# Fifth scan's decays in a tile outside layer 0's memory, second sequence's statistics ahead of the third scan, second gates in step 12, expert choice a scan later

## The chip, the core and the metric

The kernel runs on one core of a Trainium2 chip. A core has a matrix engine (TensorE, PE), a vector engine (VectorE, DVE), an engine for activation functions (ScalarE, ACT), a general engine (GpSimd, POOL) and one that mainly issues transfers (SyncE, SP). Each engine works through its own list of instructions in the order in which the program issues them; semaphores make an instruction of one engine wait for one of another. The metric is the time of one execution in device microseconds (us).

## The reference

The input x is four sequences of 256 tokens with 512 features, in float32. Two layers follow each other. Each adds to its input the sum of two branches, both fed with the layer norm of that input.

Layer 0: an attention with 32 heads over a latent of four numbers for each key, and a gated feed-forward with 1792 hidden features.

Layer 1: a selective state-space block and a mixture of experts.

```python
x, z = jnp.split(hidden_states @ in_proj_w, 2, axis=-1)
# causal convolution of four taps over time on x, then silu: xc
dt = softplus(dt_r @ dt_proj_w + dt_bias)          # dt_r, Bm, Cm: rms-normed projections of xc
h = exp(dt * A) * h + dt * Bm * xc                  # one step of time, 1024 channels x 16 states
y = sum over states of h * Cm
out = ((y + D * xc) * silu(z)) @ out_proj_w
```

The recurrence over h runs over 256 steps of time in each sequence. The expert part takes a softmax over eight experts for every token, keeps the two largest, and adds their low-rank products to a dense product.

## The kernel before

**Layer 0** is a list of TensorE work (attention and feed-forward) with the rest threaded between. Its last piece is the product of the hidden features with the down weights (`down`, L432). The generator `ff` holds this product for the last four blocks of 128 tokens; calls such as `go(ff, 9)` issue some of its matmuls at a time, so that the first steps of layer 1 run between them. The sums of the last three blocks stay in PSUM and are added to x by `add_last` (L452).

**Layer 1** works through the four sequences b = 0 to 3. Each sequence is cut into eight chunks of 128 channels (c), and each chunk into four groups of four states (g). So there are 32 steps for a sequence and 128 in all, counted by u. One step u handles 128 partitions x 4 x 256 elements:

- `decays(u)` (L877): four exponentials on ACT make the factors exp(dt * A) from the tile `dts` of the chunk.
- `scan_in(u)` (L891): DVE multiplies the spread rows of Bm with `dus` (dt times xc of the chunk) into `bx`, in PSUM, of which there is one buffer.
- `scan(u)` (L899): DVE runs the recurrence into `h`; GpSimd multiplies `h` with the rows of Cm into `hc`.
- `states_sum(u - 1)` (L919): TensorE sums `hc` over the states into `ysum`, one step later.
- `close_chunk` (L928), two steps after a chunk's last scan: DVE multiplies `ysum` with the gate `sz`.

The tiles `dts` and `dus` of a chunk come by way of a scratch tensor in HBM: `send` (L840) writes it, `spread` (L844) reads it back in the layout of the scan, both on SyncE's queue.

Around these steps stands everything that other sequences and chunks need, placed by hand. `put(b, s, f, ...)` (L1141) says that f is issued in step s of sequence b, ahead of that step's `scan_in`; `put_late` (L1144) places it after that step's `scan`. The loop at L1265 issues, for each u: the decays two steps ahead, what `put` placed, `scan_in`, `close_chunk`, `scan`, what `put_late` placed, and the sum of the step before. The order on each engine is the order of issue[...].

What the change touches:

- The decays' tiles. Steps 0 to 3 borrow memory: steps 0 and 2 use `decay[0]`, which lies in the pool `w1`, steps 1 and 3 use buffers of the weights (`lent`, L868). After the last matmul of `ff`, in step 2, `open_act` (L1123) closes layer 0's pools and opens the pool `act` in that memory, with two more decay tiles. From step 4 on `decay[u % len(decay)]` walks over the three. So step 4 takes `decay[1]` and step 5 `decay[2]`, both in the memory that layer 0 leaves. `decays(4)` is called at the end of step 2 (L1295), `decays(5)` at the start of step 3.
- The layer norm of the next sequence: `norm_stats` (L655: four instructions on DVE, then two small ones on ACT that make `rsn`), `norm_scale` (L665: `sh` on DVE, then two passes on ACT), `norm_turn`, `norm_copy`. For the second sequence the statistics stand late in step 3 and `norm_scale` in step 4 (L1209, L1210).
- The gates. `pz_mm(b, p, i)` (L852) multiplies with the z weights, `gate_silu` (L860) loads the table that has the silu, applies it to a pair of chunks and loads the table of exp and ln again. In the first sequence pair 1 has its matmuls in step 6 and its gate in step 8 (L1173, L1177).
- The step sizes dt: `step_in` (L772: `pdt` on TensorE, absolute value and relu on ACT) in steps 5 and 6 of the first sequence, `step_exp` (L787) in step 7.
- The next sequence's convolution: `px_mm` (L691), `conv_in` (L699: copy, first tap and three scaled copies on ACT), `conv_taps` (L716: three taps on DVE, three sums on GpSimd), pair after pair, two steps apart. In the first sequence the first pair's `conv_in` is in step 9, its taps in step 10.
- The weights' buffers: the tag `w_in` has three buffers that pairs of x and z weights use in turn; `load_x` and `load_z` (L1026, L1029) issue the transfers on SyncE's queue.
- The expert choice: `route_exp` (L962: maximum and difference on DVE, exp on ACT) in step 22 and `route` (L968: twenty small instructions on DVE) in step 23, of the first and third sequence, for two sequences at a time; `expert_turn` (L994: transposes on TensorE, a copy on ACT) in step 24, of the first three sequences.

Of the kernel before, what the change touches and what calls it, by code (L numbers as in the profile page):

```python
# [41 lines left out]
def block_kernel(  # L42
# [413 lines left out]
    def go(gen, n=1000):  # L456
        for _ in range(n):
            if next(gen, 1) == 1:
                break
# [169 lines left out]
    decay = []  # L629
# [210 lines left out]
    def send(n, b, p, t):  # L840
        live[n, b, p] = scr.tile([2, P, S], F32, tag=n, name=f"{n}d")
        nc.sync.dma_start(live[n, b, p].rearrange("c p t -> p c t"), t)
# [30 lines left out]
    def lend(n, u):  # L873
        tag = lent[n][u]
        return w1.tile([P, NG, S], F32, tag=tag, name=n, bufs=3 if tag == "w_in" else 1)

    def decays(u):  # L877
        b, c, g = u // PER, u % PER // NU, u % NU
        if u >= len(lent["d"]):
            da = decay[u % len(decay)]  # L880
        elif lent["d"][u] == "d":
            da = decay[0]
        else:
            da = lend("d", u)
            nc.gpsimd.memset(da[:, :, 0:1], 0.0)
        live["da", u] = da
        for k in range(NG):
            nc.scalar.activation(da[:, k, 1:], live["dts", b, c][:, k, 1:], AF.Exp,  # L888
                                 scale=aneg[:, c, k, g : g + 1])

    def scan_in(u):  # L891
        b, c, g = u // PER, u % PER // NU, u % NU
        bx = psx.tile([P, NG, S], F32, tag="bx", name="bx")
        nc.vector.tensor_tensor(  # L894
            bx, brow[g // 2][:, g % 2, :].unsqueeze(1).to_broadcast([P, NG, S]), live["dus", b, c], ALU.mult
        )
        live["bx"] = bx
# [191 lines left out]
    u, e, lw = live["u"], live["e"], live["lw"]  # L1089
# [51 lines left out]
    def put(b, s, f, *a):  # L1141
        at.setdefault(b * PER + s, []).append((f, a))

    def put_late(b, s, f, *a):  # L1144

        late_at.setdefault(b * PER + s, []).append((f, a))

    for b in range(B):
        nxt = b + 1
        if b:  # L1150
            put(b, 0, b_rows, b, 1)
            put(b, 0, spread, "du", b, 1)

            for c in range(DC):
                put(b, c // 2, out_mm, b - 1, 1, c)
            put(b, 3, out_x, b - 1, 1)
            put(b, 4, dense, b - 1, 0, 0)
            put(b, 5, dense, b - 1, 0, 1)
            put(b, 5, expert_out, b - 1, 0)
            for c in range(DC):  # L1160
                put(b, 6 + c, out_mm, b - 1, 0, c)
            put(b, 15, out_x, b - 1, 0)
        else:
            put(b, 1, one_out, 2)
            put(b, 1, one_step, 3)
            put(b, 2, one_out, 3)
            put_late(b, 2, load_z, b, 0)
            put_late(b, 2, lambda: send("dt", 0, 1, dts[0, 0][:, 2:4, :]))
            put_late(b, 2, step_x, b, 1)
            put(b, 4, load_z, b, 1)  # L1170
            for k, n in enumerate(("rl", "bw", "lb", "ow")):
                put(b, 9 + 2 * k, load_late, n)
            for p, u in ((0, 3), (1, 6)):  # L1173
                for i in range(2):
                    put(b, u, pz_mm, b, p, i)
            put(b, 4, gate_silu, b, 0)
            put(b, 8, gate_silu, b, 1)  # L1177
            put_late(b, 1, add_last, 5)
            put_late(b, 3, add_last, 6)
            put_late(b, 4, add_last, 7)  # L1180
        if b:
            put(b, 0, gate_silu, b, 0, 1)

        o = 0 if b else 3
        put(b, 1 if b else 5, step_in, b, 1, 0)
        put(b, 2 if b else 6, step_in, b, 1, 1)
        put(b, 3 if b else 7, step_exp, b, 1)
        for q in range(2):
            for k in range(3):
                put(b, 5 + o + 3 * q + k, step_out, b, 1, q, k)  # L1190
        for p in (2, 3):
            put(b, 3 * p + 2 + o, step_x, b, p)
        for c in range(2, DC):
            o = 0 if b or c < 4 else 1
            put(b, 3 if c == 2 and not b else 4 * c - 6 + o, spread, "dt", b, c)
            put(b, 4 * c - 4 + o, spread, "du", b, c)
        put(b, 10, load_z, b, 2)
        put(b, 12, load_z, b, 3)
        for p, at_i, at_g in ((2, (14, 15), 16), (3, (19, 21), 23)):
            for i in range(2):  # L1200
                put(b, at_i[i], pz_mm, b, p, i)
            if p == 3 or nxt == B:
                put(b, at_g, gate_silu, b, p)
        if nxt < B:
            o = 0 if b else 1
            if b:
                put(b, 0, norm_stats, nxt)
            else:
                put_late(b, 3, norm_stats, nxt)  # L1209
            put(b, 2 if b else 4, norm_scale, nxt)  # L1210
            put(b, 3 if b else 5, norm_turn, nxt, 0)
            (put if b else put_late)(b, 4 if b else 5, norm_copy, nxt, 0)
            put(b, 4 if b else 5, norm_turn, nxt, 1)
            (put if b else put_late)(b, 5, norm_copy, nxt, 1)
            for p in range(NP):
                put(b, 2 * p if b else (5, 6, 7, 8)[p], load_x, nxt, p)
                for i in range(2):
                    put(b, 6 + o + 2 * p + i, px_mm, nxt, p, i)
                put(b, 8 + o + 2 * p, conv_in, nxt, p)
                put(b, 9 + o + 2 * p, conv_taps, nxt, p)  # L1220
            put(b, 16 + o, conv_silu, nxt, (b, 2))
            put(b, 17 + o, pp_mm, nxt, 0)
            put(b, 18, pp_mm, nxt, 1)
            put(b, 19, pp_square, nxt)
            put_late(b, 20, pp_norm, nxt)
            put(b, 21, step_in, nxt, 0, 0)
            put(b, 22, step_in, nxt, 0, 1)
            put(b, 22, c_rows, nxt, 0)
            put(b, 23, step_exp, nxt, 0)
            put(b, 23, c_rows, nxt, 1)  # L1230
            for q in range(2):
                for k in range(3):
                    put(b, 24 + 3 * q + k, step_out, nxt, 0, q, k)
            put(b, 27, step_x, nxt, 0)
            put(b, 27, spread, "dt", nxt, 0)
            put(b, 29, spread, "du", nxt, 0)
            put(b, 30, step_x, nxt, 1)
            put(b, 30, b_rows, nxt, 0)
            put(b, 31, spread, "dt", nxt, 1)
            put(b, 23, load_z, nxt, 0)  # L1240
            put(b, 25, load_z, nxt, 1)
            for k, u in enumerate((27, 28, 29, 31)):
                put(b, u, pz_mm, nxt, k // 2, k % 2)
            if b % 2 == 0:
                for i, u in enumerate((16, 17, 18, 20)):
                    put(b, u, router, b, i)
                put(b, 22, route_exp, b)
                put(b, 23, route, b)
            put(b, 24, expert_turn, b)
            put(b, 25, dense, b, 1, 0)  # L1250
            put(b, 26, dense, b, 1, 1)
            put(b, 27, expert_out, b, 1)
        else:

            put(b, 12, expert_turn, b)
            put(b, 17, dense, b, 0, 0)
            put(b, 18, dense, b, 0, 1)
            put(b, 18, expert_out, b, 0)
            put(b, 20, dense, b, 1, 0)
            put(b, 21, dense, b, 1, 1)  # L1260
            put(b, 21, expert_out, b, 1)
# [3 lines left out]
    for u in range(total + 2):  # L1265
        if 3 <= u < total - 2:
            decays(u + 2)
        for f, a in at.get(u, ()):
            f(*a)
        if u < total:  # L1270
            if u:
                scan_in(u)
        last = u - 2
        if last >= 0 and last % NU == NU - 1:
            c = last % PER // NU
            close_chunk(last // PER, c)
            if last // PER == B - 1:
                late.append(c)
        if u < total:
            scan(u, 1 if u < total - 1 else 4)  # L1280
            if u < 2:
                decays(u + 2)
        for f, a in late_at.get(u, ()):
            f(*a)
        if late and u >= total - PER + 22:
            c = late.pop(0)
            for i in range(2):
                out_mm(B - 1, i, c)
        if 1 <= u <= total:
            states_sum(u - 1)  # L1290
        if u < 3:
            go(ff, (9, 12, 100)[u])
        if u == 2:
            open_act()
            decays(4)  # L1295
    for i in range(2):
        for c in late:
            out_mm(B - 1, i, c)
# [102 lines left out]
```

## Time and profile before

| what | value |
|---|---|
| time, median of three runs | 897.78 us (896.25 to 897.81) |
| time of the profiled execution | 898.7 us |
| its span, first to last instruction | 896.9 us |
| PE, DVE busy | 752.1 us (84%), 685.5 us (76%) |
| ACT, POOL busy | 526.3 us (59%), 490.3 us (55%) |
| scans on DVE (L909) | 129 instructions, 288.0 us |
| products bx on DVE (L894) | 128 instructions, 157.6 us |
| first scan starts at | 361.6 us |

The profile is of one execution, taken on the chip. Times in it are counted from the first instruction. In a row of a timeline stand the start, the length, the engine, the line of the program, the operation, the tile that it writes and those that it reads, the shapes, how many equal instructions are merged in the row, and in brackets how long the engine had been idle before it and what ended that. A matmul of float32 shows as two passes. The share of busy time is an average: TensorE leads it through layer 0, VectorE through most of layer 1.

### The profile page before, as it was taken

How to read it: one execution, taken by the hardware profiler on the slowest of the kernel's cores; microseconds unless marked ns; L12 is line 12 of the kernel's file. 1: busy time of each engine (PE TensorE's matmuls, PEld its weight loads, DVE VectorE, ACT ScalarE, POOL GpSimd, SP SyncE). 2: the span in 40 equal slices, each digit the busy share in tenths (PEclk: the TensorE clock that was granted, in tenths of full speed). 3: DMA queues.
4: the chain of work that ended last, by engine and by line, in shares of the span. 5: the costliest groups of instructions: out<-in, count | busy, mean ns of one | idle time of the engine just before them, and what ended most of it. 6: DMA issues, size and time to landing. Idle time of an engine off the chain costs nothing.

```text
span 896.9 us, 10459 instructions
## 1 busy us (share of the span) xinstructions
PE 752.1 (84%) x3554; PEld 433.4 (48%) x3554; DVE 685.5 (76%) x675; ACT 526.3 (59%) x1009; POOL 490.3 (55%) x377
## 2 busy tenths in 40 slices
PE   5999979999989999986885898687898768975875
PEld 3675545667556576653552444343444434422421
DVE  4595554376664423876998999999999989999996
ACT  4225445312437447588677596777686795764661
POOL 4222222001223242547966879868789749797664
PEclk9899999999999999998896999988999888899997
DMA  6232242001123141454752544432636332436200
GB/s 211 60 94 72 71 118 71 12 1 36 48 53 88 48 118 22 131 149 132 229 115 64 156 131 112 135 100 86 166 118 161 86 84 70 118 100 169 85 25 23
DMA packets 67343, 86.67 MB, mean 97 GB/s; under 512 B 12077, under 2 KB 52025, under 8 KB 66906
## 3 DMA queue, kind: packets, MB, share of 16 engines
q1 hardware_dynamic: 57930, 67.12, 26.8%
q0 software_dynamic: 9072, 18.35, 7.4%
q8 instruction: 28, 0.46, 0.2%
q10 hardware_dynamic: 288, 0.52, 0.2%
q14 instruction: 25, 0.20, 0.1%
HBM read 66.58 MB, written 10.22 MB: 86 GB/s over the span
## 4 chain that ended last, share of the span: by engine, by line
PE 39%; DVE 36%; ACT 14%; issue 5%; POOL 4%; DMA 1%; DVEq 0%; ACTq 0%; POOLq 0%
DVE h L909 21%; DVE bx L894 7%; ACT decay L888 6%; PE po L442 5%; PE pu L417 5%; PE pg L417 4%; PE sc L329 4%; PE av L371 3%; PE scT L361 3%; POOL hc L913 2%; PE pz L857 2%; PE pp L740 2%; PE px L696 2%; PE ysum L925 1%; ACT pe L363 1%
## 5 line engine op out<-in xcount | busy, mean ns | idle before, releaser
L913 POOL TENSOR_TENSOR hc<-h,cr 128x1024 f32<-128x1024 f32 (+1 forms) x131 | 302.3, 2310 | 115.1 <-DVE h L909 102.2
L909 DVE TENSOR_TENSOR_SCAN h<-decay,bx 128x1024 f32<-128x1024 f32 (+1 forms) x129 | 288.0, 2234 | 11.7
L888 ACT ACTIVATE decay<-dts,aneg 128x255 f32<-128x255 f32 x504 | 213.8, 498 | 126.4 <-DVE h L909 114.0
L925 PE MATMUL ysum<-hc,stack 128*32 128x256 f32 x1024 | 89.5, 420 | 91.5 <-POOL hc L913 91.2
L894 DVE TENSOR_TENSOR bx<-brow,dus 128x1024 f32<-128x1024 f32 x128 | 157.6, 1231 | 3.7
L429 POOL TENSOR_TENSOR hlo<-g,hhi 128x512 fp32r<-128x512 f32 x28 | 36.2, 1294 | 149.1 <-ACT hhi L428 149.1
L331 DVE TENSOR_REDUCE mpl<-sc 128x4 f32<-128x1024 f32 x64 | 77.2, 1222 | 24.1 <-PE sc L329 24.0
L925 PEld LDWEIGHTS ysum<-hc,stack 128*32 128x32 f32 x1024 | 21.7, 112 | 151.8 <-POOL hc L913 131.2
L400 POOL DMA_DIRECT2D wgu<-in_wgu x56 | 31.2, 558 | 92.5 <-PE pg L417 82.3
L363 ACT ACTIVATE pe<-scT 128x1024 f32<-128x1024 f32 x64 | 62.8, 1023 | 29.9 <-PE scT L361 29.6
L1017 PE MATMUL po<-ow,xc 128*128 128x512 f32 x128 | 71.2, 666 | 2.7 <-DVE xc L929 2.7
L857 PE MATMUL pz<-xn1T,w_in 128*128 128x256 f32 x256 | 68.5, 415 | 0.3 <-ACT dt L785 0.3
L696 PE MATMUL px<-xn1T,w_in 128*128 128x256 f32 x256 | 65.8, 406 | 0.8 <-DMA w_in<-in_inx 0.7
L696 PEld LDWEIGHTS px<-xn1T,w_in 128*128 128x128 f32 x256 | 51.4, 204 | 21.1 <-issue 11.0
L425 DVE SCALAR_TENSOR_TENSOR g<-g,pg 128x512 f32<-128x512 f32 x28 | 19.2, 685 | 52.0 <-ACT g L424 52.0
L857 PEld LDWEIGHTS pz<-xn1T,w_in 128*128 128x128 f32 x256 | 49.3, 202 | 19.0 <-issue 11.1
L428 ACT CAST hhi<-g 128x512 fp32r<-128x512 f32 x28 | 17.3, 620 | 61.9 <-DVE g L427 61.6
L417 PE MATMUL pg<-xhi,wgu 128*128 128x512 f32 x112 | 46.7, 417 | 5.4 <-issue 2.9
L417 PE MATMUL pu<-xhi,wgu 128*128 128x512 f32 x112 | 47.7, 426 | 3.1 <-issue 1.5
L442 PE MATMUL po<-wd,hhi 128*128 128x512 f32 x112 | 48.5, 433 | 0.0
L329 PE MATMUL sc<-km,qg 128*128 128x512 f32 x128 | 43.9, 424 | 3.3 <-ACT pe L363 2.8
L417 PE MATMUL pg<-xlo,wgu 128*128 128x512 f32 x112 | 44.9, 401 | 0.0
(225 smaller groups left out, 1255.2 us busy)
## 6 DMA issues: line engine op xcount, KB each, us to landing
dts<-dtd SPq DMA_DIRECT2D x124, 128.0 KB, 2.9
dus<-dud SPq DMA_DIRECT2D x124, 128.0 KB, 2.9
wgu<-in_wgu POOLq DMA_DIRECT2D x56, 256.0 KB, 2.7
w_in<-in_inz SPq DMA_DIRECT2D x16, 512.0 KB, 4.8
w_in<-in_inx SPq DMA_DIRECT2D x15, 512.0 KB, 4.3
dtd<-dt SPq DMA_DIRECT2D x15, 256.0 KB, 2.2
dud<-du SPq DMA_DIRECT2D x15, 256.0 KB, 2.3
wd<-in_wd POOLq DMA_DIRECT2D x7, 512.0 KB, 3.6
```

The costliest lines, as they stand in the source:

```text
L329: mm(sc[:, hp, :], lhsT=qs[b][:, gq, hf, qb * P : (qb + 1) * P], rhs=kms[b][:, 2 * hp : 2 * hp + 2, :], start=True, stop=True)
L331: nc.vector.tensor_reduce(mpl2[b % 2][:, qb, :, 16 + 2 * gq + hf].rearrange("p (a i) -> p a i", a=2), sc.rearrange("p a (i k) -> p a i k", ...
L363: nc.scalar.activation(pes[b, k][:, 2 * t : 2 * t + 2, :], sc, AF.Exp)
L417: mm(ps, lhsT=wgus[i][:, hc, :], rhs=xs[j][:, hc, :], start=(hc == 0 and j == 0), stop=(hc == HC - 1 and j == 1))
L442: mm(po, lhsT=hids[th][j][:, m, i * P : (i + 1) * P], rhs=wd[:, m, :], start=False, stop=(m == MC - 1 and j == 1))
L696: mm(px[:, i, :], lhsT=w[:, i, hc, :], rhs=xns[b][:, hc, :], start=(hc == 0), stop=(hc == HC - 1))
L857: mm(pz[:, i, :], lhsT=w[:, i, hc, :], rhs=xns[b][:, hc, :], start=(hc == 0), stop=(hc == HC - 1))
L888: nc.scalar.activation(da[:, k, 1:], live["dts", b, c][:, k, 1:], AF.Exp, scale=aneg[:, c, k, g : g + 1])
L894: nc.vector.tensor_tensor(bx, brow[g // 2][:, g % 2, :].unsqueeze(1).to_broadcast([P, NG, S]), live["dus", b, c], ALU.mult)
L909: nc.vector.tensor_tensor_scan(h[:, n].rearrange("p n t -> p (n t)"), da[:, n].rearrange("p n t -> p (n t)"), bx[:, n].rearrange("p n t -> ...
L913: nc.gpsimd.tensor_tensor(hc[:, n], h[:, n], crows[b][:, g, :].unsqueeze(1).to_broadcast([P, NG // parts, S]), ALU.mult,)
L925: mm(ysum[k * NB : (k + 1) * NB, :], lhsT=stack, rhs=hc[:, k, :], start=False, stop=(g == NU - 1))
```

## The change

The program computes the same with the same instructions; their places differ.

- From step 4 on the decay tiles are walked so that step 4 takes `decay[0]`, step 5 `decay[1]`, step 6 `decay[2]`. `decays(4)` is called a little earlier in step 2, after its scan, by the condition `u < 3`, and the call after `open_act` goes.
- The second sequence's statistics move from late in step 3 to the head of step 2.
- In the first sequence the matmuls of the second pair's gates move from step 6 to step 8, and their silu from step 8 to step 12.
- The loads of the next sequence's x weights, pairs 2 and 3, move from steps 7 and 8 to step 9, in the first sequence.
- The expert choice moves from step 23 to 24, the transposes behind it from 24 to 25.

```diff
     def decays(u):
         b, c, g = u // PER, u % PER // NU, u % NU
         if u >= len(lent["d"]):
-            da = decay[u % len(decay)]
+            da = decay[(u - 4) % 3]
...
-            for p, u in ((0, 3), (1, 6)):
+            for p, u in ((0, 3), (1, 8)):
                 for i in range(2):
                     put(b, u, pz_mm, b, p, i)
             put(b, 4, gate_silu, b, 0)
-            put(b, 8, gate_silu, b, 1)
+            put(b, 12, gate_silu, b, 1)
...
-            if b:
-                put(b, 0, norm_stats, nxt)
-            else:
-                put_late(b, 3, norm_stats, nxt)
+            put(b, 0 if b else 2, norm_stats, nxt)
...
-                put(b, 2 * p if b else (5, 6, 7, 8)[p], load_x, nxt, p)
+                put(b, 2 * p if b else (5, 6, 9, 9)[p], load_x, nxt, p)
...
-                put(b, 23, route, b)
-            put(b, 24, expert_turn, b)
+                put(b, 24, route, b)
+            put(b, 25, expert_turn, b)
...
             scan(u, 1 if u < total - 1 else 4)
-            if u < 2:
+            if u < 3:
                 decays(u + 2)
...
             open_act()
-            decays(4)
```

## The prediction

> **What bounds the kernel now.** I read the page's slices first: TensorE is full up to about 40% of the span (layer 0), VectorE from about 45% to the end. Then the waits of VectorE (DVE) from 355 us on, then the timelines of DVE and ScalarE (ACT) around them. I call the scans 0 to 127 by their step; "decays n" are the four exponentials that scan n reads. From step 4 on a step is one product bx (1.23 us) and one scan (2.29 us), and they follow each other every 3.65 us; so an idle microsecond of DVE there is a microsecond of the end, unless another wait takes its place.
>
> The waits of DVE from 355 us: who waits for whom, sum, times, longest.
>
> ```profile
> DVE sh L668 <- ACT rsn L652: 8.8, 1, 8.8
> DVE px L720 <- ACT xc L707: 7.0, 1, 7.0
> DVE xc L929 <- PE ysum L925: 3.8, 3, 2.3
> DVE w L956 <- ACT ex L966: 3.0, 2, 1.6
> ```
>
> Three of these four concern lines that the change moves. The timelines (start, length, instruction, idle time before it and its releaser) show what each stands on. ACT at the seam of the layers:
>
> ```profile
> 382.75 3.30 ACT L888 ACTIVATE decay<-dts,aneg 128x255 f32<-128x255 f32 x8 [9.81 <-PE po L442]
> 385.95 0.28 ACT L651 ACTIVATE rsn<-mv,eps 128x2 f32<-128x2 f32 x1
> 386.26 0.20 ACT L652 ACTIVATE rsn<-rsn 128x2 f32<-128x2 f32 x1
> 386.37 1.69 ACT L888 ACTIVATE decay<-dts,aneg 128x255 f32<-128x255 f32 x4
> 388.08 1.28 ACT L863 ACT_TABLE_LOAD   x1
> ...
> 400.70 0.47 ACT L784 ACTIVATE u<-pdt,vec 128x256 f32<-128x256 f32 x1 [2.31 <-PE pdt L779]
> ...
> 409.76 1.28 ACT L863 ACT_TABLE_LOAD   x1
> 411.06 0.60 ACT L863 ACTIVATE sz<-pz 128x512 f32<-128x512 f32 x1
> 411.67 1.28 ACT L647 ACT_TABLE_LOAD   x1
> 412.97 1.71 ACT L888 ACTIVATE decay<-dts,aneg 128x255 f32<-128x255 f32 x4
> ```
>
> DVE over the same stretch and at the expert choice:
>
> ```profile
> 386.50 0.16 DVE L668 SCALAR_TENSOR_TENSOR sh<-mv,rsn 128x2 f32<-128x2 f32 x1 [8.84 <-ACT rsn L652]
> 388.01 2.29 DVE L909 TENSOR_TENSOR_SCAN h<-decay,bx 128x1024 f32<-128x1024 f32 x1
> ...
> 416.34 1.01 DVE L720 SCALAR_TENSOR_TENSOR px<-pad,vec,px 128x256 f32<-128x256 f32 x2 [6.99 <-ACT xc L707]
> ...
> 472.50 0.20 DVE L956 TENSOR_REDUCE w<-ex 128x4 f32<-128x32 f32 x1 [1.57 <-ACT ex L966]
> ```
>
> ACT is idle 9.81 us because decays 4 go into a tile in layer 0's old memory, and layer 0's last product on TensorE (PE) ends just before 382.75. From there to the end of the first pair's convolution (xc, 416.30) ACT works almost without a pause while DVE waits 7 us for it: between 382.75 and 416.3 ACT is the bound, not DVE.
>
> [...] rsn's input was there at 377.66, and rsn ran at 385.95 behind decays 4 and 5. [...] Here the load is 1.28 us, but the next activation starts with it over (411.67+1.28 against 412.97)[...]; a gate costs 412.97 − 409.76 = 3.21 us, and I use that.
>
> **Part 1: decays 4 in the old tile, statistics ahead of scan 2.** The four statistics instructions (375.96 to 377.58, 1.62 us) now precede bx 2. Scan 2 goes from 369.49 to 371.1, scan 3 to 374.8 (ends 377.1), add, sh and bx 4 follow until 379.0. All this is inside DVE's idle stretch, so it costs nothing; without that cover it would cost 1.62. The rsn pair and decays 4 run on ACT from 372.94 (end of decays 3): rsn to 373.4, decays 4, free when scan 2 ends at 373.4, to 375.1. Thus 1.65 (half of 3.30) and 0.42 (385.95 to 386.37) leave the ACT chain that starts at 382.75. Decays 5 still wait there; from decays 7 on each waits, as before, for the scan three steps back.
>
> Scan 4 is not free at 379: its h is the first tile over layer 0's memory and in the built program waits for the same last product. It starts at 382.75 instead of 388.01. What is late next: chunk 0's product with its gate (L929). ACT does decays 5 and 6 (382.75 to 386.05), the table (1.28) and the silu (0.60): done at 387.94. So scan 5 starts at 388.3, against 392.26, and scans 6 to 8 follow at 3.65 each. This gain of 4 is no sum yet, as ACT decides again at the convolution.
>
> **Part 2: second gates in step 12, their matmuls in step 8.** From ACT's chain goes the gate, 3.21. Also its matmuls (16 passes, 395.89 to 399.61 on PE) no longer stand ahead of the second pdt, for which ACT waited 2.31. In the new order pdt follows the transposes (done by 392.1), one ysum and ACT's reading of the first pdt (393.8): done at 394.9, and ACT asks for it at 396.3. The wait goes whole.
>
> The matmuls now stand in step 8 ahead of the second half of px and ysum 7: ysum 5 to 395.5, px half to 397.5, ysum 6 to 398.1, gates 3.7 to 401.7, px half to 403.6, ysum 7 to 404.2. Chunk 1's product would have run at 402.8; it waits 1.4, and scan 9 ends at 406.8. ACT's chain is 1.65 + 0.42 + 3.21 + 2.31 = 7.59 shorter: xc ready at 416.30 − 7.59 = 408.7, still after DVE's 406.9. So the 1.4 is covered by 1.8, and the taps start 7.6 earlier.
>
> Loads: x pairs 2 and 3 take buffers that come free when those matmuls and the first px half end (401.7, and before 403.6). SyncE's queue now holds them behind the spread of dus for scans 12 to 15 (free to go when bx 7 ends, about 395.6) and rl; by the page's 4.3 us to landing they are there by 408. Pair 2 is used after the taps, past 410. Behind them stands dtd, whose data GpSimd finishes at about 411. Nothing is late.
>
> What step 12 pays: the gate stands between decays 14 and 15, where ACT idled 2.48 us for scan 12. 3.21 − 2.48 = 0.73 late; the third pair's xc was ready 0.33 before its taps (433.39 against 433.72): loss 0.4. The bounds are 0 (slack a little larger) and 3.2 (none). The silu itself is done some 1.8 us before chunk 2's product wants it.
>
> **Part 3: choice a scan later.** At its old place DVE waits 1.57 and, in the third sequence, 1.40 for ACT's ex. One step later DVE comes 3.65 us later than it did, ex is there 2 us before, and the same 4.56 us of small instructions follow. Gain 2.97. The decays that scan 23 needs were done at 466.3; GpSimd, which multiplies h, was free from 473.4 and waited 7.41 for that scan. The turn and its 0.35 us copy go behind one decays; their reader comes two steps later, and ACT waits 2 us per step there. In the second sequence only the turn moves, equally hidden.
>
> **Sum.** 7.59 − 0.4 + 2.97 = 10.2 us. After the taps DVE sets the pace, and its later waits stand on its own scans, so it carries to the end. The profiled execution took 898.7 (span 896.9): 888.5. That execution is 0.9 above the median 897.78, so 887.6 for the median.
>
> **Rivals.**
> 1. *Step 12 gives the gate back whole.* If ACT's slack there is used up (it works closer to DVE after the shift), the loss is 3.2, not 0.4: 890.4. Against: the idle times of 2.35 to 2.61 at every second decays in steps 10 to 16 are waits for scans, which shift along. Alike in size: the pdt wait stays, because the transposes come later than I put them: 2.3 less, 889.9. It has 1.4 us of room.
> 2. *The waits of the choice only change their name* (scan 23 or bx 24 waits for something else): 3.0 less, 890.6. Against: decays and h buffers are there, as above.
> 3. *It does not do what it says at the seam:* the memory under h, not decays 4, holds everything, and ACT catches up no time; only the choice gains: 894.8. For: h does wait for the same product. Against: ACT's queue after 382.75 is shorter by counted instructions.
> 4. *Slower.* The loads of pairs 2 and 3 stand at the head of SyncE's queue until step 8's matmuls are done, and hold dtd, dud and the spread that decays 16 read behind them. By my walk that must land by 427, and does at 424, with the loads released at 401.7 and 403.6 but dtd not ready before 411. For a loss beyond 0.2% the release would have to slip by 7.4 to meet dtd, 3 more to use the margin and 12 to eat the gain: some 22 us. I see nothing on PE that long.
>
> **Chances.** My forecast, 886 to 889.5: 0.67. Rivals 1 and 2, 889.5 to 892: 0.17. Better than 886 (the 0.4 does not show, small waits go along): 0.06. Rival 3 or two of the rivals together: 0.05. Slower: 0.05. The range 885.2 to 891.2 holds the first and most of the second and third. About 0.2% (1.8 us) is what a measurement tells from no change: faster 0.92, same 0.03, slower 0.05.
>
> **What would show it.** Right: rsn and decays 4 near 373 to 375; scan 4 at 382.7; chunk 0's product waiting about 1.2 for the silu; taps at about 408.7 behind a wait of 2; no wait at L784; L956 without its wait. A pause of 0.4 before the third pair's taps would confirm the price of step 12. Wrong: taps later than 410, a wait for PE at the second pdt, a wait of DVE over 1 us in steps 12 to 16, or one at bx 24.

## The result

| | before | the change |
|---|---|---|
| median, first comparison | 897.51 us (896.25 to 900.93, seven runs) | 889.07 us (885.4 to 895.42, seven runs) |
| profiled execution | 898.7 us | 889.37 us |
| its span | 896.9 us | 887.6 us |

The ratio is 0.9906, 95% interval 0.9882 to 0.9929. The change was run twice more beside the kernel before, in the comparisons of the experiments: 887.04 us, ratio 0.9856 (0.9837 to 0.9874), and 889.11 us, ratio 0.9877 (0.986 to 0.9893). The intervals of the first and the second don't meet; the last section shows what the times of single runs go with. The forecast, 887.6 us, is a ratio of 0.9887 to the 897.78 that it started from.

**Where the time went.** Both traces are cut at the same instructions (us; "taps" is the first tap on DVE of the first pair, "scan n" the start of scan n).

| stretch | before | after | difference |
|---|---|---|---|
| start to scan 0 | 361.64 | 360.90 | -0.74 |
| scan 0 to scan 5 | 30.62 | 26.69 | -3.93 |
| scan 5 to taps | 24.08 | 21.00 | -3.08 |
| taps to scan 14 | 20.13 | 20.56 | +0.43 |
| scan 14 to scan 22 | 32.17 | 31.32 | -0.85 |
| scan 22 to scan 24 | 13.42 | 11.97 | -1.45 |
| scan 24 to scan 86 | 245.12 | 245.11 | -0.01 |
| scan 86 to scan 88 | 13.24 | 11.97 | -1.27 |
| scan 88 to scan 127 | 145.29 | 144.83 | -0.46 |
| scan 127 to the end | 11.22 | 13.25 | +2.03 |

From scan 0 to scan 127 it is 10.6 us, where the forecast had 10.2. Ahead of scan 0 and after scan 127 the change touches nothing; the last section comes back to the +2.03. Nor does it touch the stretches from scan 14 to 22 and from scan 88 to 127: there two waits of the trace of before, 0.70 at L754 (462.96) and 0.36 at L929 (774.08), are absent. The five stretches that hold the edits sum to -9.3.

The waits of DVE from 355 us on, kernel after (who waits for whom, sum, times, longest):

```profile
DVE xc L929 <- PE ysum L925: 7.5, 3, 3.9
DVE h L909 <- PE po L442: 3.9, 1, 3.9
...
DVE xc L929 <- ACT sz L863: 1.2, 1, 1.2
DVE px L720 <- ACT xc L707: 0.4, 1, 0.4
```

The waits at L668 (8.8) and L956 (3.0) are gone, and so is the first pair's 7.0 at L720; the 0.4 that is left there is the third pair's. The waits for layer 0's last product (`po`) and for the first gate are those that the forecast put in place of the first. The waits for TensorE's `ysum` have doubled, from 3.8 to 7.5: a new one of 3.88 at chunk 1's product stands among them, for which the forecast had 1.4.

ACT at the seam, kernel after:

```profile
372.08 0.28 ACT L651 ACTIVATE rsn<-mv,eps 128x2 f32<-128x2 f32 x1
...
372.67 1.70 ACT L888 ACTIVATE decay<-dts,aneg 128x255 f32<-128x255 f32 x4
382.00 3.30 ACT L888 ACTIVATE decay<-dts,aneg 128x255 f32<-128x255 f32 x8 [7.63 <-PE po L442]
...
395.52 0.48 ACT L784 ACTIVATE u<-pdt,vec 128x256 f32<-128x256 f32 x1
...
407.24 0.57 ACT L707 ACTIVATE xc<-px,vec 128x256 f32<-128x256 f32 x1
```

`rsn` and decays 4 stand ahead of layer 0's end; eight exponentials (decays 5 and 6) are left behind it. ACT takes the second `pdt` without a pause, where it had waited 2.31. The convolution's `xc` is ready at 407.81.

DVE over the same stretch, kernel after, and at the choice:

```profile
382.06 2.29 DVE L909 TENSOR_TENSOR_SCAN h<-decay,bx 128x1024 f32<-128x1024 f32 x1 [3.95 <-PE po L442]
...
387.25 0.42 DVE L929 TENSOR_TENSOR xc<-ysum,sz 128x256 f32<-128x256 f32 x1 [1.18 <-ACT sz L863]
...
406.05 0.42 DVE L929 TENSOR_TENSOR xc<-ysum,sz 128x256 f32<-128x256 f32 x1 [3.88 <-PE ysum L925]
...
408.58 0.99 DVE L720 SCALAR_TENSOR_TENSOR px<-pad,vec,px 128x256 f32<-128x256 f32 x2
...
426.37 1.01 DVE L720 SCALAR_TENSOR_TENSOR px<-pad,vec,px 128x256 f32<-128x256 f32 x2 [0.35 <-ACT xc L707]
...
466.54 0.20 DVE L956 TENSOR_REDUCE w<-ex 128x4 f32<-128x32 f32 x1
```

Scan 4 waits for `po`, chunk 0's product 1.18 for the silu, the third pair's taps 0.35 for ACT, and the choice for nothing: each as forecast. The surprise is chunk 1's product at 406.05. It waits 3.88 for TensorE, and the taps follow it with no wait of their own: they come 0.77 after ACT had `xc` ready. So in this execution TensorE, not ACT, decides when the taps start.

### The profile page after: what moved, and what is told of

Read it like the earlier page. It is cut to its first block, busy times and chain, and to the rows that moved or that the text cites. A ratio compares the mean times of both kernels' runs of the same rounds, so it can differ in the third digit from the quotient of the medians.

```text
span 887.6 us, 10460 instructions
## 1 busy us (share of the span) xinstructions
PE 756.4 (85%) x3554; PEld 434.2 (49%) x3554; DVE 685.2 (77%) x675; ACT 525.8 (59%) x1009; POOL 489.9 (55%) x377
## 4 chain that ended last, share of the span: by engine, by line
DVE 39%; PE 36%; ACT 11%; POOL 6%; issue 5%; DMA 2%; SPq 0%; DVEq 0%; ACTq 0%; POOLq 0%
DVE h L909 23%; DVE bx L894 8%; ACT decay L888 5%; PE pu L417 5%; PE pg L417 4%; POOL hc L913 4%; PE sc L329 4%; PE av L371 3%; PE po L442 3%; PE scT L361 3%; PE px L696 2%; PE po L1017 2%; ACT pe L363 1%; PE ysum L925 1%; PE pqg L319 1%
## 5 line engine op out<-in xcount | busy, mean ns | idle before, releaser
L925 PE MATMUL ysum<-hc,stack 128*32 128x256 f32 x1024 | 93.0, 432 | 83.8 <-POOL hc L913 83.6
L1017 PE MATMUL po<-ow,xc 128*128 128x512 f32 x128 | 73.2, 682 | 2.2 <-DVE xc L929 2.2
```

The costliest lines, as they stand in the source:

```text
L925: mm(ysum[k * NB : (k + 1) * NB, :], lhsT=stack, rhs=hc[:, k, :], start=False, stop=(g == NU - 1))
L1017: mm(live["po", b, i], lhsT=xcs[b][:, c, i * P : (i + 1) * P], rhs=late_w["ow"][:, c, :], start=False, stop=(c == DC - 1))
```

## The experiments

All times are us from scan 0 of the same trace, because what lies before scan 0 varies by up to two microseconds (360.41 to 362.49 in the thirteen traces) with nothing changed there. The kernels of one comparison ran beside the kernel before on one chip.

| kernel | ratio (95% interval) | scan 5 | taps | scan 14 | scan 127 |
|---|---|---|---|---|---|
| before | 1 | 30.62 | 54.70 | 74.83 | 524.07 |
| statistics alone | 0.9984 (0.9972 to 0.9996) | 28.28 | 54.91 | 75.03 | 525.66 |
| tile and statistics | 0.9944 (0.9917 to 0.997) | 26.70 | 52.73 | 72.86 | 519.52 |
| silu alone | 0.9965 (0.9939 to 0.9992) | 30.62 | 51.38 | 71.96 | 520.99 |
| gates, matmuls and loads | 0.9916 (0.989 to 0.9942) | 30.62 | 49.50 | 70.06 | 517.01 |
| choice alone | 0.9986 (0.9971 to 1.0001) | 30.62 | 55.53 | 75.66 | 526.78 |
| the change, first | 0.9906 (0.9882 to 0.9929) | 26.69 | 47.69 | 68.25 | 513.45 |
| the change, second | 0.9856 (0.9837 to 0.9874) | 26.70 | 46.95 | 67.54 | 513.70 |
| the change, third | 0.9877 (0.986 to 0.9893) | 26.69 | 48.54 | 69.09 | 514.71 |
| second silu in step 10 | 0.9892 (0.9848 to 0.9936) | 26.69 | 46.94 | 67.81 | 513.01 |
| second gates' matmuls in step 9 | 0.9868 (0.9849 to 0.9886) | 26.69 | 46.94 | 68.81 | 514.86 |
| scan 4's h in borrowed memory | 0.9842 (0.9822 to 0.9862) | 26.69 | 48.60 | 69.15 | 514.86 |
| decays 5 in borrowed memory | 0.989 (0.9873 to 0.9907) | 26.01 | 45.78 | 66.36 | 513.85 |

The theory under test is the prediction's: ACT's queue from layer 0's end to the first convolution sets the taps, and each edit takes from it what was counted. The rivals are that something else holds DVE there (memory, TensorE), and that the waits only change their names.

**The statistics alone.** The kernel before, with this edit:

```diff
-            if b:
-                put(b, 0, norm_stats, nxt)
-            else:
-                put_late(b, 3, norm_stats, nxt)
+            put(b, 0 if b else 2, norm_stats, nxt)
```

> The kernel before with the second sequence's statistics alone moved to the head of step 2; decays 4 stay in layer 0's memory. Times are counted from the start of scan 0; there the first pair's taps start at 54.7 us and scan 127 at 524.1 in the kernel before. Theory (ACT's queue after the seam sets the taps): sh no longer waits, scan 4 starts some 3.5 us earlier (22.9 instead of 26.4), but ACT is only 0.42 us shorter, so the taps start at 54.3 and scan 127 at 523.7: 0.4 us in all. Rival (DVE's 8.8 us wait at sh is the loss itself): taps at 51.2 and 3.5 us in all.

The `rsn` pair ran at 373.68, and scan 4 came 3.5 earlier, scan 5 2.3 earlier. The taps did not come earlier: 54.91 against 54.70, where the theory had 54.3 and the rival 51.2. The pair took its 0.42 out of ACT's queue, but ACT waited 2.96 instead of 2.31 for the second `pdt`:

```profile
401.78 0.47 ACT L784 ACTIVATE u<-pdt,vec 128x256 f32<-128x256 f32 x1 [2.96 <-PE pdt L779]
```

TensorE was at half clock for 6.8 us just ahead of it, against 3.4 in the trace of before (the profile records the clock that TensorE is granted; read in windows of 0.25 us, it is 1.00 or 0.50 here, or a mixture of both where it changes). So the taps should move by -0.42 + 0.65 = +0.23, and they moved by +0.21. So a gain of 3.5 at scan 4 is worth nothing as long as ACT's queue behind it is as long. The ratio, 0.9984, is a little below 1; the 0.4 us that were counted would be 0.9996, the edge of its interval, and this trace (scan 127 at 525.66) does not show where more should come from.

**The tile and the statistics** (Part 1 of the change, no other):

```diff
-            da = decay[u % len(decay)]
+            da = decay[(u - 4) % 3]
...
+            put(b, 0 if b else 2, norm_stats, nxt)
...
-            if u < 2:
+            if u < 3:
                 decays(u + 2)
...
             open_act()
-            decays(4)
```

> The kernel before with the decay tiles and the statistics changed, gates and choice as before. Theory: ACT's queue after the seam is 2.07 us shorter, taps at 52.6 after scan 0 (before: 54.7), scan 127 at 522.0, 2.1 us in all, though scan 4 starts 5.3 to 6 us earlier. Rival: what scan 4 gains carries through, taps at 49, 5 to 6 us in all.

The taps come at 52.73, 1.97 earlier; Part 1's count is 2.07. Scan 5 is 3.9 earlier, so half of that is lost again ahead of the taps, as the prediction said ("no sum yet"). ACT's timeline of this kernel has the wait of the second `pdt` in its place:

```profile
397.69 0.47 ACT L784 ACTIVATE u<-pdt,vec 128x256 f32<-128x256 f32 x1 [2.36 <-PE pdt L779]
```

The end gains more than the taps, 4.55 up to scan 127: the choice's two waits for ACT sum to 1.7 in this trace instead of 3.0, and a wait of 0.70 at `nrm` (L754), which the trace of before has at 462.96, is absent. Neither line is touched by the edit.

**The silu alone**, its matmuls left in step 6:

```diff
-            put(b, 8, gate_silu, b, 1)
+            put(b, 12, gate_silu, b, 1)
```

> The kernel before with the second pair's silu alone moved, from step 8 to step 12; its matmuls stay in step 6, ahead of the second pdt. Theory (Part 2's two terms are separate): the gate's 3.21 leaves ScalarE's chain, its wait of 2.3 for the second pdt stays: taps at 54.7 - 3.2 = 51.5 us from scan 0, against 49.5 with matmuls and silu moved; a pause of about 0.4 before the third pair's taps; whole time 2.8 us less, ratio 0.997. Rival A (the matmuls' place is worth nothing, ScalarE meets the wait elsewhere): taps at 49.5. Rival B (the product held in one of three PSUM buffers from step 6 to 12 delays the convolution's matmuls): taps later than 52.5.

The taps come at 51.38, 3.32 earlier, against 3.21 counted for the gate; rival A wanted 49.5 and rival B later than 52.5. The line of ACT's timeline that decides it:

```profile
400.64 0.47 ACT L784 ACTIVATE u<-pdt,vec 128x256 f32<-128x256 f32 x1 [2.31 <-PE pdt L779]
```

The wait for `pdt` stays, to the hundredth of before, and the third pair's taps, at 430.76, wait 0.35 for ACT: that is the price of the gate in step 12. So the gate's time and the matmuls' place are two separate terms.

**The gates with matmuls and loads** (Part 2):

```diff
-            for p, u in ((0, 3), (1, 6)):
+            for p, u in ((0, 3), (1, 8)):
...
-            put(b, 8, gate_silu, b, 1)
+            put(b, 12, gate_silu, b, 1)
...
-                put(b, 2 * p if b else (5, 6, 7, 8)[p], load_x, nxt, p)
+                put(b, 2 * p if b else (5, 6, 9, 9)[p], load_x, nxt, p)
```

> The kernel before with the second gates' matmuls in step 8, their silu in step 12 and the two loads in step 9 alone. Theory: ACT loses the gate (3.21) and the wait for the second pdt (2.31) ahead of the taps: taps at 49.2 after scan 0 (before: 54.7), up to 2 us later if TensorE holds chunk 1's product; step 12 costs 0.4 more, scan 14 some 5 us earlier than before, 5.1 us in all. Rival: step 12 gives the gate back whole, taps at 49.2 but scan 14 only 2.3 us earlier, 2.3 us in all.

The taps come at 49.50, 5.20 earlier; the count is 3.21 + 2.31 = 5.52. From the taps to scan 14 it takes 20.56 instead of 20.13: the price of step 12 is 0.43, not 3.2. DVE's timeline shows why 0.3 of the 5.52 is missing:

```profile
408.06 0.42 DVE L929 TENSOR_TENSOR xc<-ysum,sz 128x256 f32<-128x256 f32 x1 [1.77 <-PE ysum L925]
...
410.60 0.99 DVE L720 SCALAR_TENSOR_TENSOR px<-pad,vec,px 128x256 f32<-128x256 f32 x2
```

Chunk 1's product waits for TensorE, and the taps then have no wait: DVE had become the later one. Up to scan 127 this kernel gains 7.06, where 5.1 were expected. Of the rest 1.4 lies at the choice, whose two waits sum to 1.5 in this trace instead of 3.0, and 0.7 at `nrm`, whose wait is absent; again neither line is touched by the edit.

**The choice alone** (Part 3):

```diff
-                put(b, 23, route, b)
-            put(b, 24, expert_turn, b)
+                put(b, 24, route, b)
+            put(b, 25, expert_turn, b)
```

> The kernel before with the expert choice in step 24 and the turn in step 25 alone. Theory: both waits for ex go and nothing takes their place: scan 24 starts 1.6 us earlier than before and scan 88 3.0 us, 3.0 us in all. Rival: the waits change their name (at scan 23, bx 24 or the turn), 0 to 0.5 us in all.

The waits of DVE for `ex` are gone, and no wait takes their place at scan 23 or bx 24. From scan 22 to scan 24 it takes 11.97 instead of 13.42, from scan 86 to 88 11.97 instead of 13.24, in sum 2.72. The whole time shows less: the medians, over 20 and 41 runs, are 897.82 and 899.82, but the ratio's interval (0.9971 to 1.0001) leaves out the 0.9967 that 2.97 would be. In the profiled execution the gain is eaten elsewhere, and scan 127 comes 2.7 later than before: 0.8 is lost ahead of the taps, 1.1 between scans 14 and 22, both before the choice, and 3.6 between scans 24 and 86. The waits of DVE from 460 to 890 us:

```profile
DVE h L909 <- POOL hc L913: 3.1, 1, 3.1
...
DVE nrm L754 <- ACT rs L652: 1.9, 1, 1.9
```

The first of these is at 618.39 (scan 58), inside the second sequence, where this edit moves only the transposes by a step. TensorE was at half clock from 595.3 for 17.1 us there, against at most 10.2 in the traces of before and of the change at that place; a matmul group `pdt` took 2.07 instead of 1.13, and ACT, GpSimd and the scan behind it were late. The three traces of the change, which hold the same edit, have no such wait: from scan 24 to 86 they take 245.1 to 245.3, as before (245.12). That the clock is to blame is an inference from this one trace.

That the two waits go is shown. How much that is worth is less sure: in the traces of "tile and statistics" and of the gates, where the choice stands at its old place, the same two stretches take 25.4 and 25.2 together, against 26.7 before and 23.9 here. There the move would have 1.5 and 1.3 left to gain, not 2.7. Why the old place costs less in those traces is left open.

**The change, once more** (two runs, in two comparisons):

> The changed kernel itself, again, beside the others of this call. Times are counted from the start of scan 0. Theory: the parts add up, so scan 4 starts at 21.2, the taps at 47.7 and scan 127 at 513.5 as in its first profile, whatever the clock does to layer 0 ahead of scan 0; where the granted clock falls to a half under the second pdt, px and ysum 7, chunk 1's product waits for TensorE by up to 3.9 us, at full clock by 1.4 (taps then at 47.1). Rival (the parts hinder each other): scan 127 beyond 515.

> The change once more, as the yardstick for the next kernel on the same chip. Theory (the gain is 10.6 us up to the last scan, and it varies with the clock granted to TensorE between steps 5 and 9): 0.986 to 0.991 of the kernel before; scan 5 at 26.7 us from scan 0; taps of the first pair between 46.9 (TensorE at full clock there) and 47.7 to 48.6 (half clock). Rival (the 10.6 was one execution's luck): above 0.993.

Scan 127 comes at 513.70 and 514.71, both under the rival's 515. Up to the taps the second run differs from the first in one place, TensorE between 388 and 400 us. TensorE's timeline, first run of the change:

```profile
393.16 2.07 PE L779 MATMUL pdt<-nrm,dtw 32*128 32x256 f32 x4
395.16 1.08 PE L925 MATMUL ysum<-hc,stack 128*32 128x256 f32 x8
396.17 3.29 PE L696 MATMUL px<-xn1T,w_in 128*128 128x256 f32 x8
...
405.34 0.64 PE L925 MATMUL ysum<-hc,stack 128*32 128x256 f32 x8
```

and the second run:

```profile
392.65 1.13 PE L779 MATMUL pdt<-nrm,dtw 32*128 32x256 f32 x4
393.71 0.64 PE L925 MATMUL ysum<-hc,stack 128*32 128x256 f32 x8
394.28 1.99 PE L696 MATMUL px<-xn1T,w_in 128*128 128x256 f32 x8
...
402.15 0.64 PE L925 MATMUL ysum<-hc,stack 128*32 128x256 f32 x8
```

The three groups take 6.44 in the first and 3.76 in the second, 2.68 more; chunk 1's product waits 3.88 in the first and 1.17 in the second, 2.71 more. The third run has a long half-clock stretch again, and the taps come at 48.54:

```profile
406.87 0.42 DVE L929 TENSOR_TENSOR xc<-ysum,sz 128x256 f32<-128x256 f32 x1 [4.74 <-PE ysum L925]
```

So with TensorE at half clock through these steps the product waits up to 4.7 and sets the taps. In the second run the stretch is over before the second `pdt` starts; the product waits 1.2, ACT sets the taps, and they come at 46.95, where the prediction has 47.07. The place of a stretch counts as much as its length: in the trace of the next experiment a short one (3.4 us from 395.65) lies over `px`, and the product waits 2.81, still covered by ACT.

**The second silu in step 10** instead of 12:

```diff
-            put(b, 12, gate_silu, b, 1)
+            put(b, 10, gate_silu, b, 1)
```

> The changed kernel with the second gates' silu in step 10 instead of 12; the matmuls stay in step 8. In the changed kernel ACT idled 3.06 us between decays 12 and 13, and the third pair's taps waited 0.35 for it behind step 12's gate. Theory: the gate costs 3.2, fits into that idle time but for 0.15, and the second pair's convolution has 0.2 to spare, so the 0.35 goes: from the taps to scan 14 20.2 us instead of 20.56. Rival: step 10 is as full as step 12, the same 0.35 or more appears at the second pair's taps.

The rival was right. The pause moves from the third pair's taps (0.35) to the second pair's (0.63), and the third pair has none; from the taps to scan 14 it takes 20.87, not 20.2. The whole time can't be told from the change's. The 3.06 of idle time that the expectation counted on came from the execution in which chunk 1's product had held DVE up; in the second run of the change ACT idles 2.34 there, as it does around step 12. A gate costs 0.4 to 0.6 in either step.

**The second gates' matmuls a step later**, and the loads with them:

```diff
-            for p, u in ((0, 3), (1, 8)):
+            for p, u in ((0, 3), (1, 9)):
...
-                put(b, 2 * p if b else (5, 6, 9, 9)[p], load_x, nxt, p)
+                put(b, 2 * p if b else (5, 6, 10, 10)[p], load_x, nxt, p)
```

> The changed kernel with the second gates' matmuls in step 9 instead of 8 and the two loads in step 10 instead of 9. They then stand behind the second half of px and ysum 7. Theory: chunk 1's product no longer waits for TensorE (3.9 us in the changed kernel's profile) and the taps start when ACT is done, 46.9 after scan 0 instead of 47.7: 0.8 us in all. Rival: the wait for TensorE moves to the next product or to px of the second pair, 0 or a loss.

In this execution TensorE's half-clock stretch was 10.2 us long, as in the first run of the change. DVE's timeline:

```profile
404.75 0.42 DVE L929 TENSOR_TENSOR xc<-ysum,sz 128x256 f32<-128x256 f32 x1 [1.39 <-PE ysum L925]
...
409.03 1.02 DVE L720 SCALAR_TENSOR_TENSOR px<-pad,vec,px 128x256 f32<-128x256 f32 x2 [1.66 <-ACT xc L707]
...
425.61 0.42 DVE L929 TENSOR_TENSOR xc<-ysum,sz 128x256 f32<-128x256 f32 x1 [1.64 <-PE ysum L925]
```

Without the gates' 3.7 us ahead of it, chunk 1's product waits 1.39 even so, and ACT sets the taps again (46.94). Chunk 2's product then waits 1.64 for the matmuls that it now has ahead of it: scan 14 comes at 68.81, no earlier than in the change. The theory's taps came as counted, but the rival is right on the whole: the wait was moved, not removed.

**Scan 4's h in borrowed memory** (hc stays where it was), so that scan 4 needn't wait for layer 0's last product:

```diff
-         "d": ("d", "w_in", "d", "w_in"), "h": ("w_in", "u", "e", "u"),
+         "d": ("d", "w_in", "d", "w_in"), "h": ("w_in", "u", "e", "u", "e"),
...
```

> The changed kernel with scan 4's h in the borrowed tile that scan 2 used, outside layer 0's memory. DVE's wait of 3.95 us for TensorE at scan 4 goes; scan 4 starts about 17.3 us after scan 0 instead of 21.2. Theory: scan 5 still waits for chunk 0's product and that for the first gate's silu, so scan 5 stays at 26.7, the taps at 47.7 and the time the same. Rival: the wait at scan 4 is on the path, scan 5 and all that follows 3 to 4 us earlier.

DVE's timeline (the program is three lines longer here, so the scan is L912 and the product L932):

```profile
379.11 2.29 DVE L912 TENSOR_TENSOR_SCAN h<-decay,bx 128x1024 f32<-128x1024 f32 x1
...
382.88 0.69 DVE L454 TENSOR_TENSOR x<-x,po 128x512 f32<-128x512 f32 x1 [1.48 <-PE po L442]
...
388.12 0.42 DVE L932 TENSOR_TENSOR xc<-ysum,sz 128x256 f32<-128x256 f32 x1 [3.41 <-ACT sz L863]
```

Scan 4 starts 17.34 after scan 0 instead of 21.16 and waits for nothing: h was what held it. Scan 5 stays at 26.69, because the addition of layer 0's last sum (L454) now waits 1.48 for `po`, and chunk 0's product 3.41 instead of 1.18 for the silu. So the memory under h costs the change nothing; the first gate's silu on ACT decides when scan 5 starts. The taps, at 48.60, are those of a trace with a half-clock stretch of 10.2 us, as in the third run of the change (48.54).

**Decays 5 in borrowed memory**, so that ACT has four exponentials instead of eight ahead of the first gate:

```diff
-         "d": ("d", "w_in", "d", "w_in"), "h": ("w_in", "u", "e", "u"),
+         "d": ("d", "w_in", "d", "w_in", "d", "e"), "h": ("w_in", "u", "e", "u"),
...
-        if 3 <= u < total - 2:
+        if 4 <= u < total - 2:
...
             open_act()
+            decays(5)
```

> The change, and decays 5 also taken out of layer 0's memory, into a borrowed tile, so that ScalarE has only decays 6 between layer 0's last product and the first gate. Theory (Part 1's counting: the exponentials that stand ahead of the first gate's silu set scan 5 and the taps): the silu would come 1.65 earlier, but the gate's own matmuls end 24.5 us from scan 0, so it comes 1.2 earlier: scan 5 at 25.5 us from scan 0 instead of 26.7, no wait of chunk 0's product for the silu, taps at 45.7 to 47 and the end 1.2 earlier than the change without it. Rival (TensorE, not ScalarE's queue, sets steps 5 to 9 once the change is made): scan 5 at 25.5, but chunk 1's product waits 1.2 longer, taps and end unchanged.

The outcome lies between theory and rival. ACT, kernel with this edit:

```profile
382.83 1.71 ACT L888 ACTIVATE decay<-dts,aneg 128x255 f32<-128x255 f32 x4 [5.19 <-PE po L442]
...
386.28 0.60 ACT L863 ACTIVATE sz<-pz 128x512 f32<-128x512 f32 x1 [0.44 <-PE pz L857]
```

The silu comes 1.2 earlier and now waits for its matmuls, as counted. Scan 5 comes 0.68 earlier, not 1.2: chunk 0's product waits 0.49 for `ysum`, whose matmuls stand on TensorE behind those of the gate (1.07 for `ysum`), an item that the expectation left out. The taps come at 45.78, 1.17 earlier than in the second run of the change (both with a half-clock stretch of 3.4 us). The end doesn't show it: 890.44 (888.68 to 891.14) against 889.11 (888.62 to 890.62) for the change on the same chip. In the profile the kernel is ahead by 1.1 at scan 22 (98.49 against 99.61) and has lost it by scan 86, to a wait of 0.95 for GpSimd at 606.19 and one of 1.65 instead of 1.10 for `ysum` at 618.77. No kernel run here is shown to beat the change.

## Why the prediction was right, and where it was off

**Part 1** held as counted: scan 4 is at 21.16 from scan 0 (forecast 21.11), scan 5 at 26.69 (26.66), chunk 0's product waits 1.18 for the silu (about 1.2). Alone, the part is worth 1.97 at the taps (2.07). That ACT's queue, not the memory under h, sets what follows is shown by two runs on the change: the one that freed h left scan 5 where it was, and the one that took decays 5 out of ACT's queue brought scan 5 0.68 and the taps 1.17 forward.

**Part 2.** The silu alone brought 3.32 (3.21 counted), silu and matmuls together 5.20 (5.52); what the matmuls add is the difference, 1.88 (2.31), as they were not moved alone. The gate's 3.21 rests on the trace of before: a load of 1.28, the silu of 0.60 and a load of 1.28 again, each followed within 0.02 by the next activation (409.76 to 412.97). The 3.32 measured is 0.11 from it. Step 12 pays 0.35 to 0.43 (0.4).

One step failed: "so the 1.4 is covered by 1.8". The wait of chunk 1's product for TensorE was 3.88, 1.17 and 4.74 in the three profiled executions of the change. The walk over TensorE's queue took every matmul at the duration that the trace of before has from 396 us on, where the clock is full; in two of three executions `pdt`, `ysum` and `px` ran at half clock and the 1.4 was 2.5 to 3.3 too small. What this adds to the taps is smaller, 0.7 to 1.6 (47.69 and 48.54 against 46.95), since 1.9 of it is covered by ACT. In "what would show it", the wait of 2 ahead of the taps is therefore missing in the first and the third execution and there in the second (1.89).

**Part 3** held in that both waits go with no wait in exchange. Its size, 2.97 forecast, was 2.72 both alone and in the change, each against the one trace of before; against the traces in which other edits had already shrunk these waits, 1.3 to 1.5 would be left. The whole times of the choice alone do not show it clear of no change.

**The sum.** Up to scan 127 the forecast had 10.2; what the parts run alone gain at their own places is 1.97 + 5.20 - 0.43 + 2.72 = 9.5; the change's first trace has 10.6, of which 0.7 is the missing wait at `nrm` that the change doesn't touch (it is back, with 0.65, in the second execution) and 0.4 the missing wait at L929 after scan 88. The stretches that hold the edits give 9.3. So the mechanism and the size hold, but that 10.2 and 10.6 lie so close is in part luck: the waits that happened to be absent, 1.3 with some tenths around them, made up for the 0.9 by which the edits' own stretches fall short. The profiled execution was forecast at 888.5 and took 889.37: 0.4 better up to scan 127, 0.74 better ahead of scan 0, 2.03 worse after scan 127; that these nearly cancel is luck as well. The ratios of the three parts multiply to 0.9944 x 0.9916 x 0.9986 = 0.985, near the 0.9856 to 0.9906 of the whole; with their intervals this is no sharp test of the sum.

**The rivals.** Rival 1 (step 12 gives back 3.2, or the `pdt` wait stays) is refuted by the 0.35 and by the absence of a wait at L784. Rival 2 fails at the choice: no new wait within two steps. Rival 3 is refuted by the taps of Part 1 alone. Rival 4 (SyncE's loads): the loads of pairs 2 and 3 are issued at 403.72, and `dtd` at 412.43, directly behind GpSimd's last product for it (411.14 + 1.26). They hold up nothing, with over 6 us to spare; "nothing is late" held.

## What to carry to other kernels

Where two engines take turns in setting the pace, an edit is worth what it takes out of the queue of the engine that sets the next meeting point, not what it moves at the first: scan 4 came 3.5 earlier with the statistics alone, and 3.8 earlier once more with h moved on top of the change, and neither brought the taps forward. Two edits to one chain (the gate, and the matmuls ahead of `pdt`) should be priced and tried apart: here they came to 3.3 and 1.9. When a wait for TensorE is said to be covered, work it out once more with its matmuls at half clock: here `pdt` took 2.07 us instead of 1.13, and the wait 3.88 instead of 1.17.

## What the runs showed of the hardware

**TensorE's half-clock stretches differ in length from trace to trace and have no fixed place in the program.** Each of the thirteen traces has exactly one stretch at half clock between 386 and 404 us: it is 3.4 us long in six (before, silu alone, tile and statistics, the change's second run, silu in step 10, decays 5), 6.8 in two (statistics, choice) and 10.2 in five (the change's first and third run, gates, matmuls in step 9, h). It begins anywhere between 388.6 and 395.7, in the same program too: 388.6, 389.2 and 390.4 in the three runs of the change. In this stretch of the change's first run, 10.2 us long, the columns are the window and its length, the busy time of PE, of weight loads, DVE, ACT and POOL, then the granted clock (third from the right), the DMA share and GB/s:

```profile
388.60:398.50 9.90, 9.10 (x36) 5.55 (x37) 9.54 (x6) 9.90 (x24) 5.85 (x3) 0.50 0.57 155
```

TensorE was busy by the profile for 9.10 of 9.90 us and stayed at half clock; from 392.01 to 395.43 it had no pause at all (3.42 busy of 3.42). So in this trace a TensorE that was busy nearly all the time ran at half clock for 10.2 us; what takes full clock away and what brings it back is not shown.

**Such a stretch moves whole microseconds at single places.** The +2.03 after scan 127 comes with such a stretch (876.7 to 883.5): 1.80 of it lies in the last product, and most of the rest in the wait for `ysum` ahead of it. In the first run of the change:

```profile
879.80 3.78 PE L1017 MATMUL po<-ow,xc 128*128 128x512 f32 x4 [0.52 <-DVE xc L929]
```

and in the second run, at full clock:

```profile
879.14 1.98 PE L1017 MATMUL po<-ow,xc 128*128 128x512 f32 x4 [0.52 <-DVE xc L929]
```

From scan 127 to the end it is 13.3 us with such a stretch over the last product (the change's first and third run, decays 5) and 11.0 to 11.5 in the other ten. Over the whole execution the change's times go with the mean granted clock: of its fifteen runs the seven with 0.934 or more took 885.4 to 888.62, the eight with less 889.02 to 895.42. It is a relation, not a cause that was shown, and it is loose for the choice alone (894.83 at 0.927, 902.25 at 0.926). Differences of one or two microseconds between two kernels here need several runs of each, and a trace cut at the same instructions.
